# Two idle products ahead of the first weights, the input rows queued later, and the gate biases loaded in the second pair's first pass

## The chip, the core and the metric

The kernel runs on one core of a Trainium2 chip. The metric is device time in microseconds (us) of one execution. The program is one launch: it reads all its inputs from the chip's memory and writes a 512 x 512 float32 result. All products are float32, so each 128x512 product shows in the trace as two matrix passes.

The engines are called by the names of the profile: PE is the matrix engine (PEld its weight loads), DVE the vector engine, ACT the scalar engine, POOL the GpSimd engine, SP the sync engine, which here only issues transfers. Three transfer queues are used: SP's own (q1 in the profile), POOL's (q0) and ACT's (q10). All three are served by the same 16 transfer engines.

## What is computed

One block of a perceiver on `x` (8 batches x 64 slots x 512) with a context `ctx` (8 x 1601 x 512): a slot attention with a gated recurrent update, then self attention, then a mixture of experts. Only the first of the three matters here:

```python
Pn = rmsnorm(ctx, input_norm_w)
k_proj, v_proj = Pn @ Wk.T, Pn @ Wv.T
slots = layernorm(x)
for _ in range(3):
    q = rmsnorm(slots, slot_norm_w) @ Wq.T
    attn = softmax(q @ k_proj.T * D ** -0.5, over the slots)
    attn = attn / (sum over the context + 1e-6)
    upd = attn @ v_proj
    gx, gh = upd @ wih.T + bih, slots @ whh.T + bhh      # three gates of 512 each
    r = sigmoid(gx_r + gh_r); z = sigmoid(gx_z + gh_z)
    n = tanh(gx_n + r * gh_n)
    slots = (1 - z) * n + z * slots
x = x + slots
```

The biases `bih` and `bhh` (1536 numbers each) enter only in the gates. For r and z only the sum of the two is needed; for n the second one stays apart, because r multiplies it.

## The kernel before

The 512 slots form four row tiles of 128, each tile a pair of batches (t = 0 to 3). The weights are folded first: `Wq` and `Wk` into `wqk` (16 products, line 174, tiles `pwqk`), and `Wv` with the three gate blocks of `wih` into `wvi[0..2]` (`fold_values`, line 621, 16 products for each block, tiles `pwvi`). Then the context is used as it comes: a pass X of a pair makes scores (`attend`, line 425, tiles `sc`) and the softmax, a pass Y (`update`, line 547) multiplies the attention with the context rows (tiles `pu`) and runs the gates.

In its first pass X a pair also makes the transposed context (`prepare`, line 353). Each 128x512 row tile is transposed on PE into a bank `tr_p`, half of it is copied out by DVE (line 375) and half by ACT (line 376), ACT also squares the rows (line 378), and each finished 512 KB half group is stored to memory (`kept`, line 386) by a transfer that POOL issues, for the later passes to read back.

The order of the stages is fixed (line 224): X of pair 0, X of pair 1, Y of pair 0, and so on; pairs 2 and 3 follow later. Pair 0's first pass is "pos 0", pair 1's first pass "pos 1", and the first update is at "pos 2". Transfers that SP issues go through `queue` (line 127), which keeps them in the order of the program text. Context tiles live in a ring of 1024-wide places (tags `nat`, `ctxT` and their halves); `pump` (line 311) issues the next load as soon as a place is free, in a planned order, and a place that held transposed columns is free only when its `kept` store has landed. At most eight transfers of a queue are outstanding at a time; the ninth issue waits for the first.

A scheduler places each engine's instructions, so the order on an engine is fixed when the program is built, and is not that of the text except where `keep_in_program_order` asks for it.

What the change touches:

- Lines 138 to 158: the first loads. ACT issues the four chunks of `wq`, SP those of `wk`, then `xall` (the input rows, 1 MB), `wv` (1 MB) and `wih_0` (1 MB). POOL issues four small vectors, among them `snw_s` and `inw_s`.
- Line 149: `qscale`, a tiny DVE instruction, DVE's first, which waits for `inw_s`.
- Lines 402 to 420: POOL issues the broadcasts of `bih` into `b_i` (768 KB), of the n part of `bhh` into `b_hn` (256 KB) and of the r and z parts into `b_h` (512 KB). DVE adds `b_h` into `b_i` (line 420).
- Lines 600 to 607 in `update`: the gates read `b_hn` and the three thirds of `b_i`.
- Lines 661 to 666: pos 1. `fold_values(2)` there reads `wv` for the last time, and `whh_2` is loaded into a place that this frees.

Of the kernel before, what the change touches and what calls it, by code (L numbers as in the profile page):

```python
# [9 lines left out]
F32 = mybir.dt.float32  # L10
# [5 lines left out]
P = 128  # L16
D = 512
DC = D // P
# [5 lines left out]
NMT = MT + 1  # L24
# [16 lines left out]
def perceiver_kernel(  # L41
# [7 lines left out]
    nc = tc.nc  # L49

    const = ctx.enter_context(tc.tile_pool(name="const", bufs=1))
# [16 lines left out]
    def chunk(name, tag="w"):  # L68

        bufs, width = SLOTS[tag]  # L70
        return big.tile([P, width], F32, tag=tag, name=name, bufs=bufs)
# [4 lines left out]
    def bank(name, tag="ring"):  # L76
        return ps.tile([P, 512], F32, tag=tag, name=name)
# [47 lines left out]
    xall = const.tile([P, NPAIR, D], F32, name="xall")  # L125

    def queue(dst, src):

        return tc.keep_in_program_order(nc.sync.dma_start(dst, src))  # L129

    def load_w(src, j, name, eng=None, dst=None):

        t = chunk3(name) if dst is None else dst
        issue = eng if eng is queue else eng.dma_start
        issue(t, src[:, ts(j, 512)].rearrange("(c p) f -> p c f", p=P))
        return t
# [6 lines left out]
    inw_s = const.tile([P, DC], F32, name="inw_s")  # L143
    with nc.allow_non_contiguous_dma(reason="two short vectors onto partitions"):
        nc.gpsimd.dma_start(snw_s, snw.rearrange("(c p) -> p c", p=P))
        nc.gpsimd.dma_start(inw_s, inw.rearrange("(c p) -> p c", p=P))
    queue(xall, x.rearrange("(t p) d -> p t d", p=P))
    qscale = const.tile([P, DC], F32, name="qscale")
    nc.vector.tensor_scalar_mul(qscale, inw_s, float(D) ** -0.5)
    rw_s = const.tile([P, DC, E], F32, name="rw_s")  # L150
    nc.gpsimd.dma_start(rw_s, rw.rearrange("(c p) e -> p c e", p=P))

# [1 line left out]
    wih_s = [chunk3("wih_0"), chunk3("wih_1")]  # L154
    wvv = load_w(wv, 0, "wv", queue)
    load_w(wihT, 0, "wih_0", queue, wih_s[0])
    rb_b = const.tile([P, E], F32, name="rb_b")
    nc.gpsimd.dma_start(rb_b, rb.partition_broadcast(P))
    ones = const.tile([P, 1], F32, name="ones")
# [2 lines left out]
    def matmul4(dst, lhsT, rhs, start=True, stop=True):  # L162
        for c in range(DC):
            last = nc.tensor.matmul(  # L164
                dst, lhsT=lhsT(c), rhs=rhs(c),
                start=start and c == 0, stop=stop and c == DC - 1,
            )
        return last


    pw = [bank(f"pwqk_{dc}") for dc in range(DC)]
    for c in range(DC):
        for dc in range(DC):
            nc.tensor.matmul(
                pw[dc], lhsT=wq_s[:, c, ts(dc, P)], rhs=wk_s[:, c, :],
                start=c == 0, stop=c == DC - 1,
# [224 lines left out]

    b_i = const.tile([P, 3 * D], F32, name="b_i")
    b_hn = const.tile([P, D], F32, name="b_hn")
    nc.gpsimd.dma_start(b_i, bih.partition_broadcast(P))
    nc.gpsimd.dma_start(b_hn, bhh[2 * D :].partition_broadcast(P))
    work = phase_pool("slot_work")
    widen("nat", SLOTS["nat"][0] - 2)
    widen("ctxT", SLOTS["nat"][0] - 2)
# [3 lines left out]
    for c, tag in enumerate(("r", "z", "sT", "quT")):  # L412
# [1 line left out]
        queue(w, wihT[ts(c, P), 2 * D :])  # L414
        wih_2.append(w)
    widen("ctxT", SLOTS["ctxT"][0] - SLOTS["nat"][0] + 2)
    b_h = work.tile([P, NMT * P], F32, tag="wide", name="b_h", bufs=3)[:, : 2 * D]
    nc.gpsimd.dma_start(b_h, bhh[: 2 * D].partition_broadcast(P))
    tc.keep_in_program_order(
        nc.vector.tensor_add(b_i[:, : 2 * D], b_i[:, : 2 * D], b_h)  # L420
    )

    slots_of, sT_of = {}, {}

# [122 lines left out]
    def update(t, it, att, banks=None, late=(), between=lambda n: None):  # L547

        n = f"{t}_{it}"
        e, part = att  # L550
        slots = slots_of[t]
        H = D // 2
        pu, rs = bank(f"pu_{n}"), bank(f"rs_{n}")
        for i in range(NMT):
            k = P if i < MT else TAIL
            for j in range(2):
                nc.tensor.matmul(  # L557
                    pu[j * S : (j + 1) * S, :],
                    lhsT=e[:k, i, ts(j, S)], rhs=row_tile("Y", t, it, j, i),
                    start=i == 0, stop=i == MT,  # L560
                )
                row_used("Y", t, it, j, i)
            if i == MT - 2:
                tc.keep_in_program_order(
                    nc.tensor.matmul(rs[:, :1], lhsT=part, rhs=ones, start=True, stop=True)
                )
        between(2)
        if banks is None:
            banks = recur(t, it)
            for c in range(DC - 1):  # L570
                recur_more(t, banks, c)
        pr, pz, phn, pxn = banks
        cs = small.tile([P, 1], F32, tag="cs", name=f"cs_{n}")
        nc.vector.tensor_scalar_add(cs, rs[:, :1], 1e-6)
        nc.vector.reciprocal(cs, cs)
        upd = work.tile([P, D], F32, tag="nat", name=f"upd_{n}", bufs=2)
        nc.vector.tensor_scalar_mul(upd[:, :H], pu[:, :H], cs)
        nc.scalar.mul(upd[:, H:], pu[:, H:], cs)

        for part_of_it in late:  # L580
            next(part_of_it)
        uT = work.tile([P, DC, P], F32, tag="quT", name=f"uT_{n}", bufs=2)
        tr_u = transpose4(upd, f"u_{n}")
        recur_more(t, banks, DC - 1)
        half = DC // 2
        nc.vector.tensor_copy(uT[:, :half], tr_u[:, :half])
        nc.scalar.copy(uT[:, half:], tr_u[:, half:])
        for part_of_it in late:
            for _ in part_of_it:
                pass  # L590
        for j, pg in enumerate((pr, pz, pxn)):
            matmul4(
                pg, lambda c: uT[:, c, :], lambda c: wvi[j][:, c, :], start=j == 2
            )
            between(4)

        r = work.tile([P, D], F32, tag="r", name=f"r_{n}")
        z = work.tile([P, D], F32, tag="z", name=f"z_{n}")
        new = work.tile([P, D], F32, tag="slots", name=f"slots_{t}_{it + 1}", bufs=4)
        nc.vector.tensor_add(new, phn, b_hn)  # L600
        nc.vector.tensor_add(r, pr, b_i[:, :D])
        nc.scalar.activation(r, r, AF.Tanh, scale=0.5)
        nc.vector.tensor_add(z, pz, b_i[:, D : 2 * D])
        nc.scalar.activation(z, z, AF.Tanh, scale=0.5)
        nc.vector.scalar_tensor_tensor(new, r, 1.0, new, ALU.add, ALU.mult)
        nc.vector.scalar_tensor_tensor(r, new, 0.5, pxn, ALU.mult, ALU.add)
        nc.vector.tensor_add(r, r, b_i[:, 2 * D :])
        nc.scalar.activation(r, r, AF.Tanh)
        nc.vector.tensor_sub(new, slots, r)
        nc.vector.scalar_tensor_tensor(new, z, 1.0, new, ALU.add, ALU.mult)  # L610
        nc.vector.scalar_tensor_tensor(new, new, 0.5, r, ALU.mult, ALU.add)
        slots_of[t] = new
        if it == ITERS - 1:
            add = nc.vector if (t, it) == trail[-1] else nc.gpsimd
            add.tensor_add(xall[:, t, :], xall[:, t, :], new)
# [26 lines left out]
    def start_group(g):  # L642
# [8 lines left out]
        elif g == 2:  # L651
            columns_to(new_pair, 2 * NMT + 1)

    att, begun, late = {}, {}, ()
    for pos, (half, (t, it)) in enumerate(stages[:-1]):
        if pos == 0:
            new_pair = t
            columns[t], tiles_done[t] = prepare(t, fold_values(0)), 0
            widen("nat", 2)
            pump()  # L660
        if pos == 1:
            new_pair = t
            columns[t], tiles_done[t] = prepare(t), 0
            fold_values(2, columns_more)
            wvi_done.append(True)
            whh_s.append(load_w(whhT, 2, "whh_2", queue))
        if half == "Y":
            more = ()
            if stages[pos + 1][0] == "X" and stages[pos + 1][1][1] == 0:

                new_pair = stages[pos + 1][1][0]
                columns[new_pair], tiles_done[new_pair] = prepare(new_pair, tag="ring"), 0
                more = (columns_more,)
            update(t, it, att.pop(t), begun.pop((t, it), None), late, *more)
            late = ()
            continue
        if it == 0:
            new_pair = t
            slots_of[t] = work.tile([P, D], F32, tag="slots", name=f"slots_{t}_0", bufs=4)
            normalised(slots_of[t], xall[:, t, :], mv0, r0, t)  # L680
            att[t], late = attend(t, it, start_group)
            if stages[pos + 1][0] == "X":
                for part_of_it in late:
                    for _ in part_of_it:
                        pass
                late = ()
            continue

        other = stages[pos + 1][1]
        begun[other] = recur(*other)  # L690
        att[t], late = attend(
            t, it, fill=lambda c: recur_more(other[0], begun[other], c)
        )
# [198 lines left out]
    mv, r = layernorm(xall[:, :2, :], "att_01", 2)  # L892
# [4 lines left out]
    mv, r = layernorm(xall[:, 2:3, :], "att_2")  # L897
# [56 lines left out]
    mv, r = layernorm(xall[:, 3:4, :], "att_3")  # L954
# [11 lines left out]
    work = phase_pool("ffn_work")  # L966
# [16 lines left out]
    for i in range(TOP):  # L983
# [26 lines left out]
        start=True, stop=True,  # L1010
# [206 lines left out]
```

## Time and profile before

| | |
|---|---|
| three runs | 964.88, 969.2 and 971.65 us, median 969.2 us |
| the profiled execution | 969.19 us, of which the span from the first to the last instruction is 967.4 us |
| PE busy | 923.2 us, 95% of the span |
| DVE, ACT, POOL busy | 419.1, 241.4, 199.1 us |
| moved to and from memory | 237.45 MB, 245 GB/s on average |
| first product (`pwqk`) | starts at 4.73 us, after waiting for `wk` |
| first product of the values' fold (`pwvi`) | starts at 22.63 us |
| first pass X of pair 1 | about 102 to 129 us |
| first pass Y of pair 0 | about 130 to 165 us |

PE is busy for 95% of the time, so the places where it is idle can be counted one by one. Times in the views count from the start of the span. A line of the timeline holds the start, the duration, the engine, the line of the code, the operation, the tiles (written <- read) and in brackets the idle time of that engine just before it and what ended it. The granted clock is the share of full speed at which PE was allowed to run.

### The profile page before, as it was taken

To read this page: it belongs to the slowest core of one execution; us is meant where nothing else is said; L and a number is where in the kernel's file an instruction comes from. 1 tells how busy PE (TensorE), PEld (TensorE's weight loads), DVE (VectorE), ACT (ScalarE), POOL (GpSimd) and SP (SyncE) were. 2 spreads that over 40 slices of the span, in tenths; PEclk is the share of its full clock that TensorE was granted. 3 is DMA by queue.
4 is the path that set the end of the run, shared out by engine and by line. 5 is a ranking of instruction groups with operands and counts; after the bars stand their busy time and mean duration, and the time that the engine had idled before them with its cause. 6 is when DMAs were issued, how large, how long until landed. Compare 5 with 4: busy or idle time off the path is not lost. (4 is left out here: it accounts for less than half of the span.)

```text
span 967.4 us, 11781 instructions
## 1 busy us (share of the span) xinstructions
PE 923.2 (95%) x4081; PEld 439.0 (45%) x4081; DVE 419.1 (43%) x1111; ACT 241.4 (25%) x594; POOL 199.1 (21%) x319
## 2 busy tenths in 40 slices
PE   7999899999999999998999999999999897998995
PEld 3545434444444445454443434343443455684442
DVE  1517344252526365545453636353521737432223
ACT  1457531111111127446111111111100113101220
POOL 2013331030303032322211112030332110041212
PEclk9999999999999999999999999999999999899998
DMA  9997797494939388969938677675844100059934
GB/s 330 382 363 284 280 394 284 172 371 137 403 114 409 105 324 294 381 209 346 394 149 306 238 271 273 246 298 198 293 158 137 54 1 1 1 196 367 370 132 153
DMA packets 85852, 237.45 MB, mean 245 GB/s; under 512 B 8558, under 2 KB 24958, under 8 KB 85792
## 3 DMA queue, kind: packets, MB, share of 16 engines
q1 hardware_dynamic: 73312, 195.45, 55.4%
q0 software_dynamic: 11328, 39.14, 10.4%
q10 hardware_dynamic: 1152, 2.10, 0.6%
q8 instruction: 33, 0.54, 0.2%
q14 instruction: 27, 0.22, 0.1%
HBM read 201.22 MB, written 36.48 MB: 246 GB/s over the span
## 5 line engine op out<-in xcount | busy, mean ns | idle before, releaser
L512 POOL TENSOR_TENSOR raw<-e,rms 128x512 f32<-128x512 f32 (+1 forms) x48 | 45.6, 959 | 404.8 <-DVE e L510 392.5
L468 PE MATMUL sc<-ring_ctxT,qT 128*64 128x512 f32 x296 | 97.0, 596 | 2.2 <-DVE qT L452 1.8
L557 PE MATMUL pu<-ring_nat,e 128*64 128x512 f32 x308 | 94.5, 596 | 0.0
L468 PE MATMUL sc<-ring_nat,qT 128*64 128x512 f32 x280 | 91.2, 594 | 0.0
L557 PE MATMUL pu<-ring_ctxT,e 128*64 128x512 f32 x268 | 86.0, 596 | 0.0
L503 DVE TENSOR_REDUCE mx<-tr_e 128x8 f32<-128x512 f32 (+1 forms) x48 | 26.8, 585 | 102.9 <-PE tr_e L491 102.5
L476 ACT ACTIVATE raw<-sc,sri 128x512 f32<-128x512 f32 (+1 forms) x48 | 27.5, 595 | 100.7 <-PE sc L468 100.7
L468 PEld LDWEIGHTS sc<-ring_ctxT,qT 128*64 128x64 f32 x296 | 28.4, 137 | 50.2 <-issue 42.9
L542 PE MATMUL pz<-whh,sT 128*128 128x512 f32 x96 | 48.0, 594 | 0.0
L164 PE MATMUL pwvi<-wih,wv 128*128 128x512 f32 x96 | 43.3, 594 | 1.6 <-DMA wih<-in_wihT 1.6
L164 PE MATMUL pab<-up_b,xT 128*128 128x512 f32 x96 | 43.2, 594 | 0.8 <-ACT xT L87 0.7
L533 PE MATMUL pr<-whh,sT 128*128 128x512 f32 x96 | 43.9, 594 | 0.0
L164 PE MATMUL pqkv<-wqkv,haT 128*128 128x512 f32 x96 | 42.2, 596 | 1.4 <-ACT haT L721 1.4
L164 PE MATMUL pq<-wqk,sT 128*128 128x512 f32 x96 | 43.5, 595 | 0.0
L557 PEld LDWEIGHTS pu<-ring_ctxT,e 128*64 128x64 f32 x268 | 24.9, 137 | 40.8 <-issue 40.5
L164 PE MATMUL pxn<-wvi,uT 128*128 128x512 f32 x96 | 43.2, 592 | 0.0
L164 PE MATMUL pr<-wvi,uT 128*128 128x512 f32 x96 | 43.2, 592 | 0.0
L164 PE MATMUL pz<-wvi,uT 128*128 128x512 f32 x96 | 43.2, 592 | 0.0
L468 PEld LDWEIGHTS sc<-ring_nat,qT 128*64 128x64 f32 x280 | 27.6, 137 | 32.7 <-issue 29.9
L557 PEld LDWEIGHTS pu<-ring_nat,e 128*64 128x64 f32 x308 | 27.7, 137 | 30.5 <-issue 28.4
L375 DVE COPY ring_ctxT<-tr_p 128x256 f32<-128x256 f32 x60 | 24.4, 421 | 35.9 <-PE tr_p L111 21.6
L378 ACT ACTIVATE ring_nat<-ring_nat 128x512 f32<-128x512 f32 x54 | 34.7, 644 | 13.7 <-PE tr_p L111 10.7
(259 smaller groups left out, 1455.1 us busy)
## 6 DMA issues: line engine op xcount, KB each, us to landing
ring_nat<-in_ctxp SPq DMA_DIRECT2D x104, 512.0 KB
ring_ctxT<-in_ctxp SPq DMA_DIRECT2D x88, 512.0 KB
ring_ctxT<-kept SPq DMA_DIRECT2D x48, 512.0 KB
ring_nat<-kept SPq DMA_DIRECT2D x48, 512.0 KB
kept<-ring_ctxT POOLq DMA_DIRECT2D x26, 512.0 KB, 7.2
up_b<-in_w SPq DMA_DIRECT2D x24, 512.0 KB
kept<-ring_nat POOLq DMA_DIRECT2D x22, 512.0 KB, 8.9
dn_b<-in_w SPq DMA_DIRECT2D x12, 512.0 KB
```

The costliest lines, as they stand in the source:

```text
L164: last = nc.tensor.matmul(dst, lhsT=lhsT(c), rhs=rhs(c), start=start and c == 0, stop=stop and c == DC - 1,)
L375: nc.vector.tensor_copy(parts[0][:, :, cols], pt[:, :2, :])
L378: nc.scalar.activation(src, src, AF.Square, accum_out=ss[:k, i, j : j + 1])
L468: nc.tensor.matmul(sc[j * S : (j + 1) * S, :], lhsT=qT[:, c, ts(j, S)], rhs=cols, start=c == 0, stop=c == DC - 1,)
L476: nc.scalar.mul(raw[:, lo:hi], sc, ri)
L503: nc.vector.reduce_max(mxr, rows3(pt), axis=AX.X)
L512: nc.gpsimd.tensor_mul(rows3(prod), ee, wide(rms))
L533: nc.tensor.matmul(banks[j], lhsT=sT_of[t][:, c, :], rhs=whh_s[j][:, c, :], start=c == 0, stop=False,)
L542: tc.keep_in_program_order(nc.tensor.matmul(banks[j], lhsT=sT_of[t][:, k, :], rhs=whh_s[j][:, k, :], start=k == 0, stop=j == 2,))
L557: nc.tensor.matmul(pu[j * S : (j + 1) * S, :], lhsT=e[:k, i, ts(j, S)], rhs=row_tile("Y", t, it, j, i), start=i == 0, stop=i == MT,)
```

## The change

It does four things.

- Two products of a zeroed tile with itself (`awake`, 128 x 512) into a bank that nobody reads (`idle`) are put ahead of the first real product. DVE zeroes the tile with a memset, which becomes its first instruction; `qscale` comes after it.
- The load of `xall` moves on SP's queue from in front of `wv` to behind `wih_0`.
- The broadcasts of `b_i` and `b_hn` move to pos 1. On POOL they now stand behind the last addition of pair 0's `part` (line 518 of the kernel before) and in front of the four `kept` stores that come next. The 512 KB of `b_h` become two loads of 256 KB on SP's queue, behind `whh_2` and in front of pair 0's next context rows; they use the tiles of `r` and `z`, which are not yet needed for the gates.
- The sum of the biases becomes two 128x512 additions on DVE, made in the first update after its softmax and ahead of its first gate instruction.

```diff
-    queue(xall, x.rearrange("(t p) d -> p t d", p=P))
-    qscale = const.tile([P, DC], F32, name="qscale")
-    nc.vector.tensor_scalar_mul(qscale, inw_s, float(D) ** -0.5)
...
     load_w(wihT, 0, "wih_0", queue, wih_s[0])
+    queue(xall, x.rearrange("(t p) d -> p t d", p=P))
...
+    awake = chunk("awake")[:, :D]
+    tc.keep_in_program_order(nc.vector.memset(awake, 0.0))
+    idle = bank("idle")
+    for n in range(2):
+        tc.keep_in_program_order(nc.tensor.matmul(
+            idle, lhsT=awake[:, :P], rhs=awake, start=True, stop=True
+        ))
+    qscale = const.tile([P, DC], F32, name="qscale")
+    tc.keep_in_program_order(nc.vector.tensor_scalar_mul(qscale, inw_s, float(D) ** -0.5))
...
-    nc.gpsimd.dma_start(b_i, bih.partition_broadcast(P))
-    nc.gpsimd.dma_start(b_hn, bhh[2 * D :].partition_broadcast(P))
...
-    b_h = work.tile([P, NMT * P], F32, tag="wide", name="b_h", bufs=3)[:, : 2 * D]
-    nc.gpsimd.dma_start(b_h, bhh[: 2 * D].partition_broadcast(P))
-    tc.keep_in_program_order(
-        nc.vector.tensor_add(b_i[:, : 2 * D], b_i[:, : 2 * D], b_h)
-    )
...
+        while b_more:
+            b, more = b_more.pop(0)
+            tc.keep_in_program_order(nc.vector.tensor_add(b, b, more))
...
+    b_more = []
...
         if pos == 1:
+            for b, v in ((b_i, bih), (b_hn, bhh[2 * D :])):
+                tc.keep_in_program_order(nc.gpsimd.dma_start(b, v.partition_broadcast(P)))
             new_pair = t
             columns[t], tiles_done[t] = prepare(t), 0
             fold_values(2, columns_more)
             wvi_done.append(True)
             whh_s.append(load_w(whhT, 2, "whh_2", queue))
+            for j, tag in enumerate(("r", "z")):
+                b_h = work.tile([P, D], F32, tag=tag, name=f"b_h_{j}")
+                queue(b_h, bhh[ts(j, D)].partition_broadcast(P))
+                b_more.append((b_i[:, ts(j, D)], b_h))
```

Elsewhere the order changes only in pos 0: DVE and ACT copy the first two transposed tiles a little earlier, and the four products of `pwvi_1_0` stand one to two transposes later on PE. From pos 1 on, each engine's order is that of before but for the moved instructions.

## The prediction

> **What bounds the kernel now.** I read the page first, then PE's waits over the whole span, then the timeline where the change acts, and last the transfer queues in the stretches where it moves bytes.
>
> ```profile
> span 967.4 us, 11781 instructions
> ...
> PE 923.2 (95%) x4081; PEld 439.0 (45%) x4081; DVE 419.1 (43%) x1111; ACT 241.4 (25%) x594; POOL 199.1 (21%) x319
> ```
>
> PE is the bound, and only its idle stretches and its slow stretches can give time back. The opening, from the timeline:
>
> ```profile
> 5.71 0.34 PEld L174 LDWEIGHTS pwqk<-wk,wq 128*128 128x128 f32 x1 [0.52 <-issue]
> 6.57 0.34 PEld L174 LDWEIGHTS pwqk<-wk,wq 128*128 128x128 f32 x1 [0.52 <-issue]
> ...
> 9.12 0.34 PEld L174 LDWEIGHTS pwqk<-wk,wq 128*128 128x128 f32 x1 [0.52 <-issue]
> 9.72 0.19 PEld L174 LDWEIGHTS pwqk<-wk,wq 128*128 128x128 f32 x1 [0.26 <-issue]
> 10.15 0.19 PEld L174 LDWEIGHTS pwqk<-wk,wq 128*128 128x128 f32 x1 [0.24 <-issue]
> ...
> 22.63 13.97 PE L164 MATMUL pwvi<-wih,wv 128*128 128x512 f32 x32 [1.58 <-DMA wih<-in_wihT]
> ```
>
> The weight loads come 0.86 us apart until 9.12 and 0.43 us apart from 9.72: PE starts at half speed. The step from 9.12 to 9.72 is 0.60, so the speed changed at about 9.46, or 4.73 us after the first product. Half of that, 2.37 us, is lost. Then PE waits 1.58 us for `wih_0`. That makes 3.95 us, all that the front can give.
>
> The place that the biases move to, in pair 1's first pass and pair 0's first update:
>
> ```profile
> 102.16 2.18 POOL L386 DMA_DIRECT2D kept<-ring_ctxT  x4
> 118.78 0.37 ACT L376 COPY ring_nat<-tr_p 128x256 f32<-128x256 f32 x1 [5.09 <-DMA kept<-ring_nat]
> 119.21 0.66 PE L111 MATMUL tr_p<-ident,ring_nat 128*128 128x128 f32 x4 [1.60 <-ACT ring_nat L376]
> 142.09 1.73 PE L557 MATMUL pu<-tail_Y,e 65*64 65x512 f32 x4 [1.19 <-DMA tail_Y<-in_ctxp]
> ```
>
> ACT waits 5.09 us until a `kept` store, POOL's fifth in this stretch, has landed. PE waits for ACT, and later for the load of `tail_Y`. So here, unlike elsewhere, transfers stand on the path. What the two queues did in two stretches (queue, packets, MB, share of 16 engines), 9 to 13 us and 106 to 118 us:
>
> ```profile
> DMA packets 521, 1.53 MB, mean 383 GB/s; under 512 B 85, under 2 KB 91, under 8 KB 521
> ...
> q0 software_dynamic: 250, 1.04, 67.5%
> q1 hardware_dynamic: 247, 0.48, 34.2%
> ```
> ```profile
> DMA packets 1498, 5.02 MB, mean 419 GB/s; under 512 B 142, under 2 KB 142, under 8 KB 1496
> ...
> q0 software_dynamic: 734, 2.69, 54.9%
> q1 hardware_dynamic: 762, 2.32, 48.0%
> ```
>
> The engines are full in both. In the first, the biases on POOL's queue take two thirds of what moves. In the second, POOL's stores get 0.22 MB/us: 2.69 MB are just over five stores of 0.524, so the fifth ends its data at 117.7 and is known to have landed at 118.7.
>
> **Idle products.** The memset can start when the other engines do (0.81). It writes 128x512; the nearest DVE rows are 0.15 us (128x1) and 0.69 us (128x512), so the products start at 1.0 to 1.5. I take 1.5, by the equal size. They are four passes of 0.86, 3.4 us, and end at 4.9: the real products begin 0.2 later than 4.73. If PE needs 4.73 us of work before full speed, it is there at 6.2. Half speed then costs the real products (6.2 - 4.9) / 2 = 0.65 in place of 2.37. Gain: 2.37 - 0.65 - 0.2 = 1.5. Bounds: -0.2 (idle products do not count) and 2.37. `qscale` behind the memset costs nothing: it waits for `inw_s` until 10.25 anyway.
>
> The Trainium skill (TensorE: Matmul & The Clock Gate, "What's actually happening") says that speed is granted after one full window of about 3.4 us of work, and that windows run free of the kernel's start. By it the change to full speed moves by one window, 3.4 / 2 - 0.2 = 1.5, or where a window edge falls badly by none, -0.2 (estimates); one profiled execution can't show how often.
>
> **Input rows and biases out of the way of `wih_0`.** SP's queue had moved 0.99 MB by 9 us and needs 3.15 (`wk`, `wv`, `wih_0`, 1.05 each) instead of 4.2. With no bias beside it, the other 2.16 MB take 5.5 us at the 0.39 MB/us of this stretch: until 14.5, and 15.9 with the 1.4 us that `wih_0` took to be seen before (4.2 MB are through at about 21.2, the product starts at 22.63). PE ends `pwqk` at 21.05 - 1.5 = 19.5, so the wait of 1.58 goes whole; bounds 1.2 and 1.58. Next late is nobody: `xall`, 1.05 MB more, is there at 18.6, when DVE, which reads it at 21.75 now, would come to it at 20.2. The chain from there to the slots ends at 29.47 now, and PE asks for them at 36.4. The `b_i` addition taken from DVE (1.23 us at 27.33) and the copies moved in pos 0 are worth nothing: DVE idles 7.60 us before `sT`, ACT 2.52 before `q`. Later loads have 1.57 MB less ahead of them, 3.9 us, more than PE gains. So PE is ahead by 1.5 + 1.6 = **3.1 us** until 102 (bounds 1.0 and 3.95).
>
> **Biases in pos 1.** On POOL, two issues (0.55 us each, by the same rows at 4.80 and 5.34) stand in front of four stores. The issues are covered by the stores' backlog; the bytes are not. The same 1.05 MB took 4.0 us of the queue between 9 and 13, beside loads of 2 KB packets as here (`whh_2`). The fifth store then lands 4.0 later, and ACT, DVE's next copies and PE behind ACT are already waiting for it: **4.0 us** on PE at 119.21. Bounds: 4.7 (1.05 MB at 0.22), and 1.4, because the engines moved only 0.52 MB between 102 and 106 where 1.6 would fit, and bias data in that hole would delay the stores by 2.6 less. I stay at 4.0: the first store's data began only at 106, the first row of its kind after ten idle microseconds, and the bias load takes that place.
>
> `tail_Y` needs all that was queued before it, now 1.57 MB more: 3.8 us at 0.41 MB/us. It is there at 142.09 + 3.8 - 3.1 = 142.8. PE comes to it at 140.90 + 4.0 - 3.1 = 141.8 and waits 1.0 instead of 1.19. `b_h`'s own two issues (0.4 each) on SP delay row loads that SP has 10 us of backlog for.
>
> **The clock in that wait.** PE's wait grows from 1.60 to 5.6 us.
>
> ```profile
> 118.00:122.00 4.00, 1.99 (x13) 1.47 (x14) 1.12 (x4) 3.22 (x10) 0.53 (x1) 1.00 1.02 419
> 767.00:770.60 3.60, 1.43 (x26) 0.84 (x24) 2.73 (x13) 0.00 (x0) 1.32 (x2) 1.00 0.00 0
> 770.60:777.50 6.90, 6.10 (x55) 4.97 (x56) 2.78 (x5) 2.31 (x4) 0.64 (x1) 0.51 0.01 2
> 821.80:825.30 3.50, 3.50 (x5) 1.38 (x5) 0.00 (x0) 0.00 (x0) 0.00 (x0) 0.51 0.01 2
> ```
>
> These are stretches: length, PE busy, ..., granted clock. 1.99 busy in 4.00 kept the full clock; 1.43 in 3.60 was followed by 6.9 us at 0.51. With almost nothing busy in 5.6 us the second row is nearer. The shortest halved stretch is 3.5 us and costs 1.7; bounds 0 and 3.4. PE then comes to `tail_Y` at 141.8 + 1.7 = 143.5, past its landing at 142.8. The same section of the skill speaks against the change here: one idle window of about 3.4 us is enough for half speed. No run here shows that threshold; by it the 1.7 is due, without it the sum is 0.7 less.
>
> **The additions in the first update.** Two of 0.69 us (the 128x512 additions of line 601) come before `r` at 158.21. DVE then waits 0.46 for `pz` and 2.74 for `pxn`: 1.4 of 3.2 us is covered. If that cover were gone, they would cost 1.4.
>
> **Sum** at 142.09: 143.5 - 142.09 = +1.4. After it PE waits for no transfer for a long time (the engines idle from 164 to 180), so it stays. The profiled execution is 969.19, the median 969.2: no correction. **970.6 us.**
>
> **Rivals.**
> - The front's gain stays: the bias bytes use the hole between 102 and 106, the stores slip by 1.4, the wait is 3.0 us and the clock holds. For it: only 0.52 MB moved there; against: POOL's queue was no faster to start. PE is then 3.1 - 1.4 = 1.7 ahead at `tail_Y`, which lands at 142.09 + 3.8 - 2.6 - 3.1 = 140.2: -1.9, **967.3**; with nothing lost in pos 1, 966.1. It decides below a slip of 3.1.
> - Slower: zeros don't raise the speed. The front gives 1.58 - 0.2 = 1.4, pos 1 takes 4.0 + 1.7, less the 1.19 of the old `tail_Y` wait: +3.1, **972.3**. For it: no row here has idle products. It decides if the first real weight loads are still 0.86 apart up to about 9.5.
> - The clock holds through the wait: only `tail_Y` counts, 142.8 - 142.09 = +0.7, **969.9**. For it: 1.99 busy in 4.00 held.
>
> **How the numbers follow.** Forecast 0.40, clock holds 0.20, gain stays 0.23, zeros don't count 0.12, something unseen 0.05. The bounds of the front (1.0 to 3.95) and of pos 1 (1.4 to 4.7, clock 0 to 3.4) give 966.1 to 973; three runs of before lie 6.8 us apart, so I open the lower end: 965.5 to 973.0. One per cent is 9.7 us, about what a measurement of this kernel can tell from no change. No case reaches it; only the unseen can: faster 0.03, within 0.93, slower 0.04.
>
> **What would show it.** Real weight loads 0.43 apart from about 6; `pwvi` at 19.5 with no wait; PE 3.1 us earlier at its first `tr_e`; then the `tr_p` wait near 116 grown to over 5 us, the clock near 0.5 after it, `pu<-tail_Y` at about 143.5, the gates unchanged in length. Wrong, if that wait stays under 3 us, or if later stages shift otherwise than the `tail_Y` product does.

## The result, and the profile after

The changed kernel takes 971.87 us (median of 20 runs, 969.84 to 977.47), the kernel before 969.5 us (median of 20 runs, 964.88 to 974.7). The ratio is 1.0033, with a 95% interval of 1.0017 to 1.0049: slower by 0.33%, some 3 us, and within the one per cent that the forecast set. The profiled execution of the changed kernel took 973.81 us, 1.9 above its median; that of the kernel before, 969.19 us, was at its own. So the two traces lie 4.6 us apart where the medians lie 2.4 apart.

```profile
span 972.0 us, 11791 instructions
...
PE 928.6 (96%) x4085; PEld 441.6 (45%) x4085; DVE 418.5 (43%) x1113; ACT 241.3 (25%) x594; POOL 199.5 (21%) x318
```

The front, from the timeline:

```profile
1.54 3.78 PE L173 MATMUL idle<-awake 128*128 128x512 f32 x4 [1.54 <-DVE awake L170]
4.92 0.53 PEld L183 LDWEIGHTS pwqk<-wk,wq 128*128 128x128 f32 x2 [1.18 <-DMA wq<-in_wq]
6.82 0.34 PEld L183 LDWEIGHTS pwqk<-wk,wq 128*128 128x128 f32 x1 [0.52 <-issue]
7.42 0.19 PEld L183 LDWEIGHTS pwqk<-wk,wq 128*128 128x128 f32 x1 [0.26 <-issue]
7.84 0.19 PEld L183 LDWEIGHTS pwqk<-wk,wq 128*128 128x128 f32 x1 [0.24 <-issue]
19.86 13.90 PE L162 MATMUL pwvi<-wih,wv 128*128 128x512 f32 x32
```

The real weight loads are 0.43 us apart from 7.42 on, where before it was from 9.72 on. By the step of 0.60 from 6.82 to 7.42 the speed changed at about 7.2, which is 5.6 us after the first idle product (before, 4.73 us after the first product). `pwvi` starts at 19.86 with no wait (22.63 after a wait of 1.58). PE is 2.8 us ahead, and still is at the second `tr_s` (99.18 against 102.00).

The kernel before, after its wait for `tail_Y`, and at its next pass:

```profile
143.74 2.84 PE L533 MATMUL pr<-whh,sT 128*128 128x512 f32 x6
...
178.51 0.64 PE L468 MATMUL sc<-ring_ctxT,qT 128*64 128x512 f32 x1
```

The changed kernel in pair 1's first pass and pair 0's first update, from the timeline:

```profile
99.24 0.60 POOL L670 DMA_DIRECT2D b_i<-in_bih  x1
100.37 2.12 POOL L395 DMA_DIRECT2D kept<-ring_ctxT  x4
119.40 0.37 ACT L385 COPY ring_nat<-tr_p 128x256 f32<-128x256 f32 x1 [8.53 <-DMA kept<-ring_nat]
119.82 1.11 PE L111 MATMUL tr_p<-ident,ring_nat 128*128 128x128 f32 x4 [5.04 <-ACT ring_nat L385]
121.28 1.97 PE L111 MATMUL tr_p<-ident,ring_nat 128*128 128x128 f32 x8 [0.34 <-ACT ring_nat L385]
145.34 1.63 PE L559 MATMUL pu<-tail_Y,e 65*64 65x512 f32 x4 [3.07 <-DMA tail_Y<-in_ctxp]
146.90 4.54 PE L535 MATMUL pr<-whh,sT 128*128 128x512 f32 x6
...
183.36 0.64 PE L470 MATMUL sc<-ring_ctxT,qT 128*64 128x512 f32 x1
```

The wait of the transposes grew from 1.60 to 5.04 us, and the four transposes after it take 1.11 us where they took 0.66. The wait for `tail_Y` grew from 1.19 to 3.07, and the six passes of `pr` after it take 4.54 us (2.84 before). The granted clock says why (stretch, length, busy time of PE, PEld, DVE, ACT and POOL, granted clock, DMA share, GB/s); after each of the two waits it is well below 1:

```profile
116.00:120.00 4.00, 0.18 (x1) 0.18 (x2) 0.00 (x0) 0.60 (x2) 0.53 (x1) 0.97 1.03 422
119.00:123.00 4.00, 2.83 (x12) 2.28 (x12) 0.85 (x2) 3.60 (x12) 0.32 (x1) 0.60 1.03 420
142.00:146.00 4.00, 0.93 (x5) 0.30 (x4) 0.00 (x0) 0.00 (x0) 1.69 (x4) 1.00 1.02 299
146.00:150.00 4.00, 4.00 (x7) 1.44 (x7) 0.48 (x1) 0.47 (x1) 0.00 (x0) 0.64 1.03 397
```

The balance of the profiled execution, against the same instructions of before: -2.83 us until the wait, +3.44 in it, +0.76 at the slow transposes, +1.88 at `tail_Y`, +1.60 at the slow products. The sum is +4.85, and the next pass starts that much later (first `sc` at 183.36 instead of 178.51). At the last `py_s` products the difference is 4.16.

### The profile page after: what moved, and what is told of

Its sections match the earlier page's. It is cut to its first block, busy times and chain, and to the rows that moved or that the text cites. A ratio compares the mean times of both kernels' runs of the same rounds, so it can differ in the third digit from the quotient of the medians.

```text
span 972.0 us, 11791 instructions
## 1 busy us (share of the span) xinstructions
PE 928.6 (96%) x4085; PEld 441.6 (45%) x4085; DVE 418.5 (43%) x1113; ACT 241.3 (25%) x594; POOL 199.5 (21%) x318
## 5 line engine op out<-in xcount | busy, mean ns | idle before, releaser
L559 PE MATMUL pu<-ring_nat,e 128*64 128x512 f32 x308 | 94.5, 596 | 0.0
```

Of the source, the lines that this page charges most:

```text
L559: nc.tensor.matmul(pu[j * S : (j + 1) * S, :], lhsT=e[:k, i, ts(j, S)], rhs=row_tile("Y", t, it, j, i), start=i == 0, stop=i == MT,)
```

## The experiments

The theory: the front's gain is real and is kept. The loss comes from the bias bytes in a stretch in which transfers set the pace, and from the clock that is halved after the waits they cause. The rival: PE that arrives earlier only waits longer for transfers that take as long as before, so that the front is worth nothing wherever the biases are. Below, "the next pass" is the first `sc` after that update, at 178.51 us before and 183.36 in the changed kernel.

**Front only.** The idle products and the later `xall` are kept; the biases and their sum stay where the kernel before has them.

```diff
+    nc.gpsimd.dma_start(b_i, bih.partition_broadcast(P))
+    nc.gpsimd.dma_start(b_hn, bhh[2 * D :].partition_broadcast(P))
...
-            for b, v in ((b_i, bih), (b_hn, bhh[2 * D :])):
-                tc.keep_in_program_order(nc.gpsimd.dma_start(b, v.partition_broadcast(P)))
...
-                queue(b_h, bhh[ts(j, D)].partition_broadcast(P))
```

> Idle products and the later input rows as in the change; the bias loads and their addition stay at the front as before. Theory (the bias bytes in pair 1's first pass eat the gain): pwvi starts at 19.9 to 20.1 (wih_0 is needed at 19.86 and, with 3.15 MB ahead of and in it and the biases beside it, lands at about 19.9), the transposes' wait stays at 1.6 and the tail_Y wait at 1.2, no halved clock, first product of the next pass at 175.8 instead of 178.5: 2.7 us faster than before, ratio 0.997. Rival (PE only comes earlier to transfers that set the pace anyway): the two waits grow to 2.9 and 2.5 or so and the ratio is 1.000.

> The same kernel as in the first experiment (idle products and later rows, biases at the front), timed once more beside the rows with the stores, since its interval of 0.9967 to 1.0010 left it open. Theory: 2.5 us gained at the front and kept at the next pass, ratio 0.9975; first sc at 176.0. If the ratio comes out at 0.999 again, the gain is diluted after 760 us.

The first time 967.52 us, ratio 0.9989 (0.9967 to 1.0010); the second 966.61, ratio 0.9971 (0.9952 to 0.9990). From the timeline of the first:

```profile
19.77 4.49 PE L162 MATMUL pwvi<-wih,wv 128*128 128x512 f32 x10
...
116.76 0.66 PE L111 MATMUL tr_p<-ident,ring_nat 128*128 128x128 f32 x4 [2.04 <-ACT ring_nat L385]
139.58 1.74 PE L567 MATMUL pu<-tail_Y,e 65*64 65x512 f32 x4 [1.14 <-DMA tail_Y<-in_ctxp]
141.26 2.84 PE L543 MATMUL pr<-whh,sT 128*128 128x512 f32 x6
```

The waits are near those of before (2.04 us for 1.60, 1.14 for 1.19), the products are at full speed, and the next pass starts at 176.03 and 176.09, 2.4 to 2.5 us earlier than before. The rival falls: with the biases loaded at the front, `pwvi` still does not wait, and PE keeps most of its lead (2.9 us at the second `tr_s`, 2.5 at the next pass). So with `xall` behind `wih_0` the biases need not move.

**Biases only.** The biases and their sum are moved as in the change; no idle products, `xall` in its old place.

```diff
-    awake = chunk("awake")[:, :D]
...
+    queue(xall, x.rearrange("(t p) d -> p t d", p=P))
```

> The bias loads and additions moved as in the change, no idle products, input rows in front of wv as before. Theory: wih_0 has no biases beside it, 4.2 MB of the queue end at about 17.2 and land at 18.6, before PE needs them at 21.05, so the 1.58 us wait goes; in pair 1's first pass the transposes' wait is 5.0 and that for tail_Y about 3.0, both followed by 3.4 us at half the clock; the next pass begins at 178.5 - 1.6 + 7.6 = 184.5. About 6 us slower than before, ratio 1.006. Rival (PE being ahead is what makes the waits): waits of 3.3 and 1.5, ratio 1.000 to 1.002.

976.07 us, ratio 1.0060 (1.0036 to 1.0084).

```profile
121.17 1.11 PE L111 MATMUL tr_p<-ident,ring_nat 128*128 128x128 f32 x4 [4.83 <-ACT ring_nat L378]
...
146.09 2.19 PE L552 MATMUL pu<-tail_Y,e 65*64 65x512 f32 x4 [1.51 <-DMA tail_Y<-in_ctxp]
148.21 3.97 PE L528 MATMUL pr<-whh,sT 128*128 128x512 f32 x6
```

The long first wait and both slow stretches are there without the idle products and with `xall` in its old place: the loss belongs to the biases. Without them at the front `pwvi` didn't wait either (21.44), so PE was 1.3 us ahead at the second `tr_s` here, and the next pass comes 5.6 us late, at 184.10.

**Biases behind the stores.** The whole change, but POOL issues `b_i` and `b_hn` after all the `kept` stores of this stretch.

```diff
+            if new_pair == 1:
+                for b, v in ((b_i, bih), (b_hn, bhh[2 * D :])):
+                    tc.keep_in_program_order(nc.gpsimd.dma_start(b, v.partition_broadcast(P)))
...
-            for b, v in ((b_i, bih), (b_hn, bhh[2 * D :])):
-                tc.keep_in_program_order(nc.gpsimd.dma_start(b, v.partition_broadcast(P)))
```

> The change, but POOL issues b_i and b_hn behind all twelve kept stores of pair 1 instead of in front of them; b_h as in the change. Theory (the order on POOL's queue makes the first wait, the bytes the second): the transposes' wait falls from 5.0 to about 2 (only b_h's 0.5 MB and SP's 2 KB packets in front), no halved clock after it; tail_Y still has 1.57 MB more ahead of it than before, so its wait is 3 to 5 us and the clock is halved after that; next pass at about 181, ratio 1.001. Rival (any 1.57 MB in this stretch costs the same): next pass at 183, ratio 1.003 as the change.

974.19 us, ratio 1.0042 (1.0018 to 1.0066).

```profile
115.49 0.66 PE L111 MATMUL tr_p<-ident,ring_nat 128*128 128x128 f32 x4 [1.15 <-ACT ring_nat L385]
...
143.70 2.56 PE L559 MATMUL pu<-tail_Y,e 65*64 65x512 f32 x4 [5.98 <-DMA tail_Y<-in_ctxp]
146.19 4.54 PE L535 MATMUL pr<-whh,sT 128*128 128x512 f32 x6
```

Now the transposes hardly wait, and the delay is all at `tail_Y`: 5.98 us, with the halved clock behind it. The order on POOL's queue decides where PE waits; the bytes decide most of how much. The next pass starts at 182.65, nearer to the 183 of that run's rival than to the 181 expected.

**Sums late.** Only `b_h` (0.52 MB, on SP behind `whh_2`) stays in pos 1; `b_i` and `b_hn` are loaded at the front.

```diff
+    nc.gpsimd.dma_start(b_i, bih.partition_broadcast(P))
+    nc.gpsimd.dma_start(b_hn, bhh[2 * D :].partition_broadcast(P))
...
-            for b, v in ((b_i, bih), (b_hn, bhh[2 * D :])):
-                tc.keep_in_program_order(nc.gpsimd.dma_start(b, v.partition_broadcast(P)))
```

> The changed kernel with b_i and b_hn (1.05 MB on the queue of POOL) back at the front; only b_h (0.52 MB, on the queue of SP behind whh_2) is still loaded in the second pair's first pass, and the sums are still in the first update. Theory (each byte brought into that stretch delays what stands behind it): 0.52 MB at the 0.36 to 0.38 MB per us seen there is 1.4 us; the waits of the transposes stay near 2 and 0.8 us, the wait for tail_Y is about 2.5 us, first sc of the next pass at about 177.5 (176.0 where no bias is moved, 183.4 with all); ratio 1.000. Rival (only the place on the queue of POOL costs): the wait for tail_Y stays at 1.1, the first sc comes at 176.0, ratio 0.999.

971.14 us, ratio 1.0016 (0.9993 to 1.0040).

```profile
140.63 2.61 PE L561 MATMUL pu<-tail_Y,e 65*64 65x512 f32 x4 [3.56 <-DMA tail_Y<-in_ctxp]
143.18 4.13 PE L537 MATMUL pr<-whh,sT 128*128 128x512 f32 x6
```

`tail_Y` is there 1.05 us later than with the front alone, but the wait is now 3.56 us and the clock is halved after it: `pu` and `pr` together take 2.2 us longer. The next pass starts at 179.23, 3.2 us after that of the front alone, for a third of the bias bytes. The expectation had the bytes and missed the clock, which costs twice as much here.

The four kernels give the price of the bytes. This table is worked out from the queues' totals between the issue of `whh_2` and the `tail_Y` product:

```
kernel              bias MB   MB moved   us     GB/s
front only          0         15.13      40.3   375
sums late           0.52      15.60      41.9   372
behind the stores   1.57      16.64      44.8   372
the change          1.57      16.78      46.0   365
```

Against the front alone 0.52 MB costs 1.6 us (0.33 MB/us), 1.57 MB behind the stores 4.5 us (0.35), and 1.57 MB as the change orders them 5.7 us (0.28). At the 0.375 MB/us of the front alone 1.57 MB would take 4.2 us.

**Filler products.** The whole change, with five idle products ahead of the transposes that wait and three ahead of the `tail_Y` products, so that PE is not idle before them.

```diff
+                    if (t, j, i) == (1, 1, 8):
+                        idle_products(5, "idle_x")
...
+                if (t, it, i, j) == (0, 0, MT, 0):
+                    idle_products(3, "idle_y")
```

> The change with idle products put into the two waits of PE: five (4.3 us) ahead of the transposes that wait, three (2.6 us) ahead of the tail_Y products; they write a bank that nobody reads. Theory (the waits' clock penalty is a part of the loss, some 0.8 us after the first wait and 1.6 after the second): no clock of 0.5 in 115 to 165, pr after tail_Y takes 2.8 instead of 4.5, the next pass begins at 183.4 - 2.4 = 181.0, ratio 1.001. Rival (the clock costs nothing, transfers set the pace): next pass at 183.4, ratio 1.003.

974.09 us, ratio 1.0030 (1.0007 to 1.0052), the same as the change.

```profile
120.29 0.66 PE L111 MATMUL tr_p<-ident,ring_nat 128*128 128x128 f32 x4 [1.59 <-ACT ring_nat L394]
...
147.13 1.08 PE L570 MATMUL pu<-tail_Y,e 65*64 65x512 f32 x4
148.14 3.70 PE L544 MATMUL pr<-whh,sT 128*128 128x512 f32 x8
```
```profile
120.00:124.00 4.00, 2.91 (x16) 2.10 (x16) 1.27 (x3) 4.00 (x14) 0.53 (x1) 0.80 1.03 421
124.00:128.00 4.00, 3.62 (x13) 1.60 (x14) 1.01 (x3) 3.77 (x15) 1.60 (x3) 0.50 1.02 416
```

The products after both waits are at full speed. But the wait left over (1.59 us) and the thin transposes after it bring a halved clock a little later, from about 123 to 129, where PE has dense work, and `tail_Y` is reached at 147.13. What the filler saves it loses there. Three idle products then run from 144.36, and `tail_Y` follows them without a wait, so here PE sets that time and not the transfer: in the changed kernel the data were there at 145.34. One `pr` product also moved behind `tail_Y` in this kernel (eight passes, not six). The next pass starts at 183.77. So this run does not part the price of the clock from that of the transfers; it shows only that idle products put into the waits gained nothing.

**The two parts of the front.** Idle products alone (with the old order of loads), and `xall` behind `wih_0` alone (without idle products).

```diff
+    for n in range(2):
+        tc.keep_in_program_order(nc.tensor.matmul(
+            idle, lhsT=awake[:, :P], rhs=awake, start=True, stop=True
+        ))
```
```diff
-    queue(xall, x.rearrange("(t p) d -> p t d", p=P))
...
+    queue(xall, x.rearrange("(t p) d -> p t d", p=P))
```

> The kernel before with the idle products alone; the input rows stay ahead of wih_0, the biases stay at the front. Theory (the transfers set when the fold starts): the weight loads run 0.43 us apart from 7.2 on as in the changed kernel, but wih_0 still lands near 22.6, so the wait at the first pwvi grows from 1.58 to about 2.8 us and the first pwvi stays at 22.6; everything later is as before; ratio 1.000. Rival (the idle products give the whole gain of the front by themselves): first pwvi at 21.4 with a wait of 1.6, ratio 0.9988.

> The kernel before with the input rows loaded behind wih_0, and nothing else: no idle products, the biases at the front. Theory: the wait at the first pwvi (1.58 us) is gone and the first weight loads stay 0.86 us apart until about 9.1; the first pwvi starts at 21.0 to 21.4, PE is some 1.4 us ahead until 102, and keeps it: first sc of the next pass at about 177.1 against 178.5 in the kernel before; ratio 0.9985. Rival (PE that comes earlier waits longer for the stores and for tail_Y): the waits there grow by 1.4 us and the first sc of the next pass stays at 178.5; ratio 1.000.

Idle products alone: 970.45 us, ratio 0.9999 (0.9975 to 1.0023).

```profile
22.48 7.94 PE L162 MATMUL pwvi<-wih,wv 128*128 128x512 f32 x14 [3.02 <-DVE bnst_in L199]
```
```profile
22.00:26.00 4.00, 3.52 (x5) 1.54 (x6) 3.52 (x17) 0.00 (x0) 0.00 (x0) 0.64 1.03 410
```

PE only waits longer, 3.02 us, and its clock is halved after that: the second `tr_s` comes at 103.58, 1.6 later than before, and the next pass at 180.62 (this profiled execution, 973.55 us, was 3.1 above its median). The view names a DVE instruction as what ended the wait; in the changed kernel `pwvi` starts at 19.86, before DVE's first `bnst_in` (20.73), so it does not need that one. That it waits for `wih_0`, as before, is argued from the time, not shown. The idle products are worth nothing unless the loads come earlier too. `xall` later, alone: 967.73 us, ratio 0.9972 (0.9952 to 0.9993); `pwvi` at 21.13 without a wait, the next pass at 177.35. The expectation had 177.1. In between, its clock was halved too, after waits of 2.01 and 0.80 us.

**Stores out of POOL's queue.** Ahead of the `kept` stores of pair 1 the transfer queues stand almost empty for some microseconds, while POOL reduces and four stores wait behind that. With the front alone the DMA share is 0.01 from 90 to 96 us and 0.22 from 96 to 102; in the kernel before it is 0.40 from 90 to 96 and 0.01 from 96 to 99. With the front alone ACT issues the four; then with the rows alone; then with the whole change.

```diff
-                    nc.gpsimd.dma_start(dst, c)
+                    early = (t, g, j) in ((1, 0, 1), (1, 1, 0))
+                    (nc.scalar if early else nc.gpsimd).dma_start(dst, c)
```

> The front of the changed kernel with the biases left where the kernel before has them (as in the first experiment), and four of the second pair's kept stores issued by ACT, not by POOL. In the first experiment the queues carry almost nothing from 90 to 101 us (DMA share 0.01 and 0.22), while the four stores wait on POOL's queue behind its reductions until 99.3; their data are written by 95 (two) and 98.4 (two). Theory (the bytes from 99 to 140 set the waits there): two stores, 1.05 MB, now go at about 95, through an empty stretch, so the stretch ends 2 to 2.8 us earlier; the waits of 2.04 and 0.80 us before the transposes and of 1.14 us before tail_Y shrink to 1 to 2 us in sum, first sc of the next pass at about 173.5 (176.0), ratio 0.996. Rival (the pace is set by when each ring place comes free, not by the bytes): the waits stay within 0.5 us, ratio 0.999.

> The two edits that gave time so far and no other: the input rows behind wih_0, and four of the second pair's kept stores issued by ACT; no idle products, all biases as in the kernel before. Theory: the gains add, 1.2 us (first sc of the next pass at 177.4 with the rows alone, 178.5 before) and 2.2 us (173.8 against 176.0): first sc near 175.1, ratio 0.996. What would show them not to add: first sc at 176 or later. A ratio of 0.998 or more with the first sc at 175.1 says that the halved-clock stretches after 760 us, whose number differs from run to run, hide a gain of this size.

> The changed kernel whole, with the four kept stores issued by ACT, so that two of them (1.05 MB) leave in the empty stretch at about 95. Theory (bytes from 99 to 145 set the pace): 1.05 MB less is 2.3 us, as in the experiment with the stores on ACT. The transposes' wait falls from 5.04 to about 2.5 us and the halved clock after it goes; the data of tail_Y land near 143.0 (145.3), PE waits 3 to 4 us for them and its clock is halved after that; first sc of the next pass at 181.0 (183.4), ratio 1.0015. Rival (the biases keep their price whatever else leaves early, since they stand on POOL's queue): the waits stay at 5.0 and 3.1, first sc at 183.4, ratio 1.0035.

The traces did about as the theory said. With the front alone the next pass starts at 173.80 (176.03 without), with the rows at 174.56 (177.35), with the change at 180.35 (183.36), where the transposes no longer wait and `tail_Y` does:

```profile
140.71 2.63 PE L560 MATMUL pu<-tail_Y,e 65*64 65x512 f32 x4 [5.55 <-DMA tail_Y<-in_ctxp]
143.27 5.14 PE L536 MATMUL pr<-whh,sT 128*128 128x512 f32 x6
```

The times did not follow: 968.38 us (ratio 0.9985, 0.9961 to 1.0009), 969.65 (0.9987, 0.9972 to 1.0002) and 976.31 (1.0063, 1.0046 to 1.0079; five runs). The last is 4.4 us above the changed kernel without this edit, though its next pass starts 3.0 us earlier. Some of the gain is given back at the very end. From the end of the last `out` issue to the end of the span the three take 6.9, 7.3 and 7.3 us, all others 2.7 to 3.2. Beside it, the rows with the stores on ACT (first) and the changed kernel (second; span 972.0), whose last issue ends at 968.94:

```profile
core 0 of [0], span 970.0 us
...
957.30 5.38 ACTq L1183 DMA_DIRECT2D out<-xall  x4
```
```profile
964.61 4.33 ACTq L1187 DMA_DIRECT2D out<-xall  x4
```

**Two stores on SP.** To tell the queue from the stores: the front alone, with two of the stores, which are ready at 94.5, issued by SP ahead of `whh_2`; SP has nothing else to do from 80 to 99.

```diff
+                    if (t, g, j) == (1, 0, 1):
+                        early.append((dst, c))
...
+            for dst, c in early:
+                queue(dst, c)
```

> The front of the changed kernel with all biases at the front (as in the first experiment), and the two kept stores whose data are written by about 95 issued by SP ahead of the load of whh_2, where SP stands idle from 80 to 99 us; ACT issues no store. With the stores on ACT the trace was ahead by 3.9 to 4.7 us at the second phn, but the span after the last products was 21 to 21.9 us against 16.9 to 17.5, so the gain was given back at the end. Theory (the 4 us at the end belong to ACT's queue, which then carried four more transfers; the 2.2 us at the stores are real): first sc of the next pass near 173.8, the time after the first py_s of the last group back to about 17 us, time near 964.5, ratio 0.995. Rival (the end costs 4 us whatever queue the stores move to): first sc near 173.8, ratio 0.9985 as before. Second rival (the stores on SP push the loads behind them later by as much): first sc at 176.

966.15 us, ratio 0.9970 (0.9954 to 0.9986), the lowest median of all, below both kernels. But the front alone, timed the second time, had 0.9971: the times do not show what the two stores add to it.

```profile
94.50 1.07 SPq L129 DMA_DIRECT2D kept<-ring_ctxT  x2
...
115.38 0.66 PE L111 MATMUL tr_p<-ident,ring_nat 128*128 128x128 f32 x4 [0.57 <-ACT ring_nat L387]
137.28 1.67 PE L572 MATMUL pu<-tail_Y,e 65*64 65x512 f32 x4 [0.21 <-DMA tail_Y<-in_ctxp]
```

The waits are 0.57, 0.81 and 0.21 us (2.04, 0.80 and 1.14 with the front alone), the next pass starts at 173.65, 4.86 us before that of the kernel before, and the end is 3.1 us after the last issue. Both rivals of this run fall: with stores on SP the end is as short as elsewhere, and the loads behind the stores are not late. This run moved two stores where the others moved four, so it does not say whether ACT's queue or the number makes the 4 us. The time fell less than the expected 964.5.

## Why the prediction was right

The forecast was 970.6 us, the measured median 971.87, inside the range and slower by less than one per cent, as the likeliest case had it. Its mechanism held as far as the first wait: lead, loss in pos 1, halved clock. At `tail_Y` it did not: a wait and a second halved stretch came there that it had at nothing.

- **Idle products, 1.5 us.** Here 1.2 us (2.77 less the wait of 1.58). In ten profiles with them the end of `pwqk` lies between 18.85 and 20.32, in four without between 21.05 and 21.61. The size was about right on average (19.71 against 21.36), and the end differs among the ten by as much as the gain itself. The sign named beforehand, loads 0.43 apart from about 6, came at 7.42.
- **Wait for `wih_0`, 1.58 us, gone.** Right. But the step took both loads out of the way, and the runs show that either is enough: `pwvi` doesn't wait with only `xall` moved (21.13), nor with only the biases moved (21.44). The second was not tried together with the idle products.
- **Transposes' wait, +4.0 us.** It was +3.44; right to within 0.6.
- **Clock after it, 1.7 us.** It was halved, as the nearest row said, but cost 0.76: PE was waiting for ACT's copies among these transposes anyway (a second wait of 0.81 us before, 0.34 after), so that half speed lost less.
- **`tail_Y`, there at 142.8.** This is the step that failed: it was there at 145.3. The 1.57 MB were priced at 0.41 MB/us, the rate from 106 to 118 us, 3.8 us; in this order they cost 5.7. Two things are in the difference. The whole stretch moves at less than that part of it: at the 0.375 MB/us of the table the price is 4.2. And the rate fell to about 240 GB/s for 3.6 us (views below); against the 420 of the front alone that is another 1.5 us, an estimate. With the lead of 2.83 in place of 3.1 this makes up the 2.5 us but for some tenths.
- **PE past its landing, no wait of weight.** It follows from the two wrong sizes: PE came at 142.27, not 143.5, and waited 3.07 us instead of none. A second halved stretch came with that, +1.60 us, which the forecast did not have. By its own sign ("later stages shift otherwise than the `tail_Y` product does") this part is wrong: the product shifts by 3.25 us, the next pass by 4.85.
- **Additions in the first update.** Right: two of 0.64 us in front of `r`, and nothing later moves by them. DVE still waits 2.19 us for `pxn` (2.74 before):

```profile
163.06 1.28 DVE L600 TENSOR_TENSOR b_i<-b_i,b_h 128x512 f32<-128x512 f32 x2
164.26 0.68 DVE L606 TENSOR_TENSOR r<-pr,b_i 128x512 f32<-128x512 f32 x1
...
169.63 0.69 DVE L611 SCALAR_TENSOR_TENSOR r<-slots,pxn 128x512 f32<-128x512 f32 x1 [2.19 <-PE pxn L162]
```

In the trace the changed kernel loses 4.85 us up to the next pass, in the runs 2.4 by the medians and 3.0 by the means (972.62 against 969.62). The forecast of 1.4 came near the time because the runs show less than the trace; that is luck, since the path it added up was short by 3.4 us at the next pass. A part of it is that the profiled execution of the changed kernel was 1.9 us above its median. The rest is not settled. It is of the size by which executions of one kernel differ after 760 us (below), and the lowest times, 969.84 and 964.88, differ by 5.0.

Of the rivals, "the front's gain stays" falls by the waits of 5.04 and 3.07; "zeros don't raise the speed" falls by the weight loads at 7.42; "the clock holds" falls by the 0.60 and 0.64.

## What to carry to other kernels

Before a load is moved out of the way, look at the DMA share in the place it goes to, not only at whether the data are needed late. Here the biases were no obstacle in the old place once `xall` was out of the way, and cost 5.7 us in the new one, while 1 MB of stores moved into an empty stretch brought the next pass 2.4 us forward in the trace (the times don't show it). And price a wait with what follows it: one of over 3 us took another 0.8 to 3.2 us through the halved clock.

## What the runs showed of the hardware

**The clock after waits.** Apart from the very first, seven waits of PE were over 3 us long (3.02 to 5.98), two in the change and one in each of five other kernels, and each was followed by a halved stretch. Shorter ones went both ways: 2.04 and 0.80 us (front only) kept the full clock, 2.01 and 0.80 (rows alone) did not, nor did 1.51 (biases only). One wait late in the kernel is alike in all fourteen profiles, 2.34 us for POOL before the first `pv`: the four passes after it took 1.05 to 1.12 us in five of them, 0.66 in seven, and 0.81 and 0.89 in the other two. The Trainium skill (TensorE: Matmul & The Clock Gate, "What's actually happening") states that half speed comes after at least one idle window of about 3.4 us, and that windows run free of the kernel. These runs are harsher: two of the seven waits (3.02 and 3.07) are shorter than such a window, and by an estimate from that figure one that runs free would seldom lie whole within a wait of 3.56. It seems that a stretch with a little work in it counts as idle too; how little is enough was not measured.

**Executions of one kernel.** After 760 us, where small products wait for other engines, the number of halved stretches differs. The two profiled executions of the front-only kernel are 0.06 us apart at the next pass (176.03 and 176.09) and 0.63 at the second group of `pv` (793.54 and 794.17), but 4.02 at the first `py_s` (835.80 and 839.82). Two kernels with the same products there differ in the same way. Front only (first) and the stores on ACT (second; this profiled execution, 974.7 us, was 6.3 above its median):

```profile
768.00:774.00 6.00, 5.56 (x60) 4.50 (x60) 2.87 (x5) 2.39 (x4) 0.05 (x1) 0.72 0.01 3
774.00:780.00 6.00, 5.38 (x133) 4.67 (x133) 2.04 (x4) 1.70 (x3) 1.26 (x1) 1.00 0.01 3
```
```profile
768.00:774.00 6.00, 5.84 (x59) 4.42 (x59) 2.97 (x5) 2.66 (x5) 0.00 (x0) 0.52 0.02 3
774.00:780.00 6.00, 6.00 (x94) 5.42 (x93) 2.13 (x4) 0.70 (x2) 1.12 (x1) 0.50 0.00 0
780.00:786.00 6.00, 4.81 (x42) 3.32 (x41) 0.00 (x0) 1.45 (x3) 0.15 (x1) 0.50 0.01 3
```

The stores on ACT were 4.1 us ahead of the kernel before at the first group of `pv` (767.22 against 771.29), and 1.7 behind at the second (799.33 against 797.61): 5.8 us lost there, more than the 4.7 won by the next pass. Of 35 runs of the kernel before in one comparison, the fastest had a mean granted clock of 0.995 and took 962.36 us, the slowest 0.981 and 975.94. A gain of some us is hard to read in such times; whether this also makes it smaller, as it seems with 4.86 us in the trace and 0.3% in the times, stays open.

**Broadcast loads.** When `b_i` and `b_hn` stand first in POOL's queue, the rate falls to about a half for some 3.6 us; with the same loads behind the stores it is full at that time. From 99 to 111 us, in slices of 0.3 us, the change (first) and the biases behind the stores (second):

```profile
GB/s 0 27 0 0 27 89 143 164 287 382 382 437 362 430 437 410 307 273 225 116 191 116 232 314 300 171 300 341 430 410 430 430 389 389 458 369 416 444 396 423
```
```profile
GB/s 0 0 0 102 41 20 20 41 61 280 321 396 403 437 444 423 403 382 444 396 458 396 382 437 430 417 389 423 430 410 464 382 232 300 321 375 430 321 307 410
```

The dip to 116 GB/s in the first is at 104 to 107 us, and the run with the biases only has one too; the smaller one in the second, to 232 at about 109, stands in the run with the sums late too, which moves only `b_h`, and not with the front alone. Why the rate falls beside these loads was not tried; at the front the same loads went at a total of 383 GB/s.

**The end of the program.** With four more transfers on ACT's queue the time after the last issue was 4 us longer, in three kernels of three; with two on SP's it was not. The profile has no row for that time; what it is stays open.
